# The seam between two attention layers: transposes, statistics and norm in another order, group values picked by a mask, and five unread products

## The chip, the cores and the metric

The kernel runs on one core of one Trainium2 chip. The metric is the device time of one execution in microseconds (us); lower is better. Three runs of the kernel before are known, and one more execution was profiled; the trace of that one gives every start time and duration below. Engines are named as the profile names them: PE is TensorE's matrix products (PEld its weight loads), DVE is VectorE, ACT is ScalarE, POOL is GpSimd, SP is the engine whose queue issues the transfers. A number like 1976.33 is a start in us from the beginning of the span.

## The reference

The input x has 128 rows of 256 positions with 256 channels. Two layers follow each other, and each adds an attention to its own input.

```python
# layer 0
x = x + L0(_gn(x), z, mask, ...)   # layer norm, 8 heads, bias from z, a gate, output product
# layer 1
x = x + L1(_gn(x), w_in, b_in, w_out, b_out, 16)  # 4 heads, keys within 16 positions

def _gn(v, G=32, eps=1e-5):
    B_, H_, W_, C_ = v.shape
    g = v.reshape(B_, H_, W_, G, C_ // G)
    m = jnp.mean(g, axis=(1, 2, 4), keepdims=True)
    s = jnp.var(g, axis=(1, 2, 4), keepdims=True)
    return ((g - m) / jnp.sqrt(s + eps)).reshape(v.shape)
```

What matters here is `_gn` ahead of layer 1. Its mean and variance are taken over all rows and positions of layer 0's output, for each of 32 groups of 8 channels. So no product of layer 1 can use its normalized input before the last row of layer 0 is known.

## The kernel before, in words

**Layer 0** works on pairs of rows, p from 0 to 63, in one loop in which four pairs are in flight: `now` (scores, exponentials, products with the values), `was` (gate, inverse sums, normalization), `old` (its second output row) and the pairs being loaded. Within a part of the code that is written under `manual_schedule` (the loop of layer 0 with its ending is one, layer 1 another), each engine runs its instructions in the order in which they are written. Between the parts a scheduler decides: in the built program the memsets of layer 1's accumulators, the constant masks, and also the two transposes at the head of layer 1 stand elsewhere than written. A finished output row is evicted by `keep_row` (line 1498), which adds the residual and writes it into `xo`, a tile of eight rows; when `xo` is full it is stored to DRAM (L1504), in x1. For each group of evicted rows `moments_of` puts work in a list, `later`: sixteen statistics instructions on DVE (L1519), and a merge of five small ones into the running statistics `st1` (L1528 to L1532). `some(n)` takes n entries off that list. The last eight rows form groups of four, two and two rows.

After the loop the last pair is still to be finished. The lines are `apply` (L1436 and L1444, products with the values and the sums of the exponentials), `gate` (L1451), `invert` (L1457), `spread` (L1475: TensorE spreads the inverse sums over the partitions, both rows in one PSUM tile), `normalize_last` (L1478), and then `out_row` (L1491) and `keep_row` for both rows. All statistics and merges that are left run after the last eviction.

**The seam.** `load_first` (L1559), issued within the loop, loads the first two rows of x1 into the memory of wq and wk, which layer 0 no longer needs. `turn` (L1901), written at the head of layer 1 but placed at 1963.91 and 1969.77 among layer 0's last instructions, transposes them into the memory of wv and wg, so that the first pair of layer 1 needs no load of its own behind the last store. `norm1` then does the norm: a product with the averaging matrix `avg` gives the mean of every group over the partitions (L1843); DVE forms the variance (L1853 to L1855); `spread_groups` copies each group's value to its eight channels (L1846), and four products with a single column (L1848) bring mean and variance to one value per partition for both halves of the channels; DVE adds the epsilon (L1858), POOL takes the power -0.5 (L1859), DVE forms nM1, the negative mean times that (L1860). `centre` (L1909) on ACT applies both to the transposed input, half by half.

**Layer 1** starts with a plain projection of pair 0 (L1984, L1999), with `nxt.centre` of pair 1 between its q and k evictions on ACT. Pair 1 and the later pairs are loaded from x1 (L1889, L1894) on SP's queue, transposed on DVE (L1904) and centred on ACT. The loop then overlaps a pair's attention with the next pair's projection by a method with seven products (L1956, L1960) whose operands are differences that POOL forms (L1922 to L1925). POOL also adds the bias to the residual (L1915) and masks the exponentials (L2024).

**The end.** The kernel also proves that its simplified arithmetic was allowed: `look` puts two half checks in a list, a maximum (L2128) and a comparison with its minimum (L2125, L2126). `some_checks(n)` takes n halves off the list, and the result is a verdict (L2288) by which a general kernel, which is not run here, would be chosen. Before the verdict stand the last pair's two output rows, evicted on DVE (L2100) and stored (L2106).

Of the kernel before, what the change touches and what calls it, by code (L numbers as in the profile page):

```python
# [9 lines left out]
F32 = mybir.dt.float32  # L10
# [763 lines left out]
def fast_kernel(  # L774
# [469 lines left out]
    class Pair:  # L1244
# [225 lines left out]
        def spread(self):  # L1470

            self.ps_rv = ps_s.tile([P, 2, KC, I], F32, name="ps_rv", tag="s")
            for r in range(2):
                for c in range(KC):
                    nc.tensor.matmul(self.ps_rv[:, r, c, :], head[:, r * KC + c, :], self.rv, start=True, stop=True)  # L1475

        def normalize_last(self, r):
            nc.vector.tensor_tensor(self.oT[r], self.oT[r], self.ps_rv[:, r], ALU.mult)  # L1478
# [75 lines left out]
    def load_first():  # L1554

        by_block = x1[0][0:2].rearrange("s (i b) (k j a) -> k j b (s i) a", b=D0, k=KC, a=D0)
        for k in range(KC):
            for j in range(HQ):
                nc.sync.dma_start(  # L1559
                    first[k][j * D0 : (j + 1) * D0].rearrange("b (i a) -> b i a", a=D0), by_block[k, j]  # L1560
                )

# [134 lines left out]
    with tc.manual_schedule():  # L1697
        old = was = Nobody()
        es = nn3 = None
        for p in range(NP):  # L1700
# [82 lines left out]
            old, was, now, nxt, nn = was, now, nxt, nn, nn3  # L1783
        was.apply(1, es)
# [3 lines left out]
        was.spread()  # L1788
        old.keep_row(1)
        for r in range(2):  # L1790
            was.normalize_last(r)
        for r in range(2):
            was.out_row(r)
            was.keep_row(r)
# [30 lines left out]
    with tc.tile_pool(name="l1", bufs=2) as sb, tc.tile_pool(  # L1825
# [11 lines left out]
        each = head.rearrange("p n d -> p (n d)").rearrange("p (n c) -> p n c", n=2)  # L1837
        wst = sb.tile([P, 4, 3, P], F32, name="wst", bufs=1)

        def norm1():  # L1840

            ps = [mm1("ps_gn") for _ in range(2)]
            nc.tensor.matmul(ps[0][:, :G], avg, st1[:, :, 1], start=True, stop=True)  # L1843

            def spread_groups(n, of):
                nc.vector.tensor_copy(each[:, n].rearrange("p (g e) -> p g e", e=GE), bcast(of, 2, GE))  # L1846
                for k in range(KC):
                    nc.tensor.matmul(  # L1848
                        ps[1][:, 2 * n + k : 2 * n + k + 1], each[:, n, k * P : (k + 1) * P], avg[:, 0:1],
                        start=True, stop=True,  # L1850
                    )

            nc.vector.tensor_tensor(dev, st1[:, :, 1], ps[0][:, :G], ALU.subtract)  # L1853
            nc.vector.tensor_mul(dev, dev, dev)
            nc.vector.scalar_tensor_tensor(dev, st1[:, :, 2], 1.0 / (S * NB * GE), dev, ALU.mult, ALU.add)  # L1855
            spread_groups(1, dev)
            spread_groups(0, st1[:, :, 1])
            nc.vector.tensor_scalar_add(R1c, ps[1][:, 2:4], 1e-5)  # L1858
            nc.gpsimd.tensor_tensor(R1c, R1c, mhalf[:, :KC], ALU.pow)  # L1859
            nc.vector.scalar_tensor_tensor(nM1, ps[1][:, 0:2], -1.0, R1c, ALU.mult, ALU.mult)  # L1860
# [15 lines left out]
        for n in range(2):  # L1876
            nc.vector.memset(o_eo[n], 0.0)
# [270 lines left out]
        with tc.manual_schedule():  # L2148
# [4 lines left out]
            for k in range(KC):  # L2153
                now.centre(k)
# [199 lines left out]
```

## Time and profile before

| what | us |
|---|---|
| median of three runs | 3128.2 (3127.22, 3128.6, 3128.2) |
| the profiled execution's own time | 3127.13 |
| its span, first to last instruction | 3125.4 |
| PE busy | 3014.3, 96% of the span |
| last eviction of layer 0 (L1498) starts | 1975.61 |
| store of the last eight rows (L1504) issued | 1976.33 |
| first product of the norm (L1843) | 1982.61 |
| nM1 (L1860) starts | 1987.17 |
| first centring (L1909) | 1987.42 |
| layer 1's first product (L1984) | 1988.29 |
| verdict (L2288) | 3118.46 |

The profiled execution's own time and its span differ by 1.7 us, which lie before the first and after the last instruction. The page gives busy times over the whole span; the stretch that the change touches is some 40 us of 3125, so it has to be read from the chain of waits (what the last instruction was released by, step by step), from the timeline (instructions in order of time, equal ones merged, with the idle time before them and what ended it) and from the table of windows (busy time, granted TensorE clock and DMA share of given stretches).

### The profile page before, as it was taken

To read this page: it belongs to the slowest core of one execution; us is meant where nothing else is said; L and a number is where in the kernel's file an instruction comes from. 1 tells how busy PE (TensorE), PEld (TensorE's weight loads), DVE (VectorE), ACT (ScalarE), POOL (GpSimd) and SP (SyncE) were. 2 spreads that over 40 slices of the span, in tenths; PEclk is the share of its full clock that TensorE was granted. 3 is DMA by queue.
4 is the path that set the end of the run, shared out by engine and by line. 5 is a ranking of instruction groups with operands and counts; after the bars stand their busy time and mean duration, and the time that the engine had idled before them with its cause. 6 is when DMAs were issued, how large, how long until landed. Compare 5 with 4: busy or idle time off the path is not lost.

```text
span 3125.4 us, 80592 instructions
## 1 busy us (share of the span) xinstructions
PE 3014.3 (96%) x33638; PEld 2097.3 (67%) x33638; DVE 2398.2 (77%) x4008; ACT 1575.7 (50%) x2639; POOL 2268.6 (73%) x1633
## 2 busy tenths in 40 slices
PE   5689999999999999999999999899999999999998
PEld 4355555566555556555555655688888888888886
DVE  7986677777777777777777777688878777777788
ACT  3454444444444444444444444355555555555553
POOL 3469899888889989888898987455555555555553
PEclk9799999999999999999999999999999999999999
DMA  9952433433333332333343332543434344444441
GB/s 359 390 180 52 99 72 97 99 68 91 91 99 71 98 99 68 91 91 99 70 98 99 64 94 68 118 97 90 97 90 96 91 96 91 95 92 93 94 95 50
DMA packets 690774, 327.90 MB, mean 105 GB/s; under 512 B 538624, under 2 KB 639872, under 8 KB 689248
## 3 DMA queue, kind: packets, MB, share of 16 engines
q1 hardware_dynamic: 686000, 320.02, 40.5%
q8 instruction: 266, 4.36, 0.6%
q10 hardware_dynamic: 4400, 2.63, 0.3%
q14 instruction: 108, 0.88, 0.1%
HBM read 253.83 MB, written 68.74 MB: 103 GB/s over the span
## 4 chain that ended last, share of the span: by engine, by line
PE 92%; DMA 4%; DVE 2%; POOL 1%; ACT 1%; issue 0%; SPq 0%; ACTq 0%; POOLq 0%; DVEq 0%
PE ps_p L1364 21%; PE ps_qk L1960 13%; PE ps_sc L1401 9%; PE ps_ov L1436 8%; PE ps_su_y L2092 7%; PE ps_y L1491 7%; PE ps_qk L1956 7%; PE ps_v L1382 7%; PE ps_o L2038 4%; PE ps_su L1444 3%; PE ps_sc L2013 3%; PE ps_su_y L2046 2%; DMA zt<-in_z_dram 2%; DMA xa<-in_x_dram 1%; PE ps_t L1143 1%; DVE st L1199 1%
## 5 line engine op out<-in xcount | busy, mean ns | idle before, releaser
L1425 POOL TENSOR_TENSOR eboth<-e 128x512 f32<-128x512 f32 x512 | 743.9, 1474 | 176.9 <-PE ps_su L1444 97.7
L1421 DVE TENSOR_TENSOR e<-ps_sc,eb 128x1024 f32<-128x1024 f32 x384 | 458.4, 1222 | 292.8 <-ACT ps_sc L1413 292.7
L1413 ACT ACTIVATE ps_sc<-ps_sc 128x1024 f32<-128x1024 f32 x384 | 375.5, 1007 | 438.7 <-PE ps_sc L1401 313.0
L1401 PE MATMUL ps_sc<-qT,kT 32*128 32x256 f32 x4096 | 294.8, 401 | 0.0
L1923 POOL TENSOR_TENSOR dT<-xgT,dT 128x256 f32<-128x256 f32 x63 | 46.1, 731 | 314.3 <-ACT xgT L1909 314.3
L2024 POOL TENSOR_TENSOR e<-e,bw 128x384 f32<-128x384 f32 x256 | 248.4, 1001 | 10.8 <-ACT e L2022 10.8
L2092 PE MATMUL ps_su_y<-w_out,oT 128*128 128x256 f32 x1008 | 254.5, 385 | 0.9 <-DVE sums L2063 0.9
L1401 PEld LDWEIGHTS ps_sc<-qT,kT 32*128 32x128 f32 x4096 | 185.9, 184 | 102.0 <-issue 91.4
L1491 PEld LDWEIGHTS ps_y<-wo,oT 128*128 128x128 f32 x1024 | 194.3, 190 | 87.6 <-issue 44.3
L1491 PE MATMUL ps_y<-wo,oT 128*128 128x256 f32 x1024 | 243.0, 380 | 6.6 <-POOL oT L1481 5.8
L1364 PE MATMUL ps_p<-xnT,wq 128*128 128x512 f32 x512 | 247.5, 605 | 0.1
L1436 PE MATMUL ps_ov<-e,v 128*32 128x256 f32 x4096 | 247.6, 382 | 0.0
L1364 PE MATMUL ps_p<-xgT,wg 128*128 128x512 f32 x512 | 247.3, 605 | 0.0
L1382 PE MATMUL ps_v<-wv,xnT 128*128 128x256 f32 x1024 | 241.8, 379 | 0.0
L1364 PE MATMUL ps_p<-xnT,wk 128*128 128x512 f32 x512 | 240.7, 592 | 0.0
L1382 PEld LDWEIGHTS ps_v<-wv,xnT 128*128 128x128 f32 x1024 | 194.5, 190 | 54.0 <-issue 30.9
L2069 DVE RECIPROCAL rv<-sums 128x256 f32<-128x256 f32 x128 | 223.1, 1743 | 0.1
L1969 ACT ACTIVATE u<-ps_qk,bin_c 128x256 f32<-128x256 f32 x378 | 174.9, 477 | 94.6 <-PE ps_qk L1960 94.6
L2092 PEld LDWEIGHTS ps_su_y<-w_out,oT 128*128 128x128 f32 x1008 | 181.8, 190 | 22.4 <-DVE sums L2063 1.3
L1436 PEld LDWEIGHTS ps_ov<-e,v 128*32 128x32 f32 x4096 | 120.0, 109 | 108.5 <-issue 41.8
L1364 PEld LDWEIGHTS ps_p<-xnT,wk 128*128 128x128 f32 x512 | 97.2, 190 | 122.8 <-issue 122.6
L1922 POOL TENSOR_TENSOR dT<-xgT 128x256 f32<-128x256 f32 x63 | 46.0, 730 | 183.2 <-ACT xgT L1909 183.2
(229 smaller groups left out, 6602.6 us busy)
## 6 DMA issues: line engine op xcount, KB each, us to landing
xa<-in_x_dram SPq DMA_DIRECT2D x8, 4096.0 KB
xt<-in_x_dram SPq DMA_DIRECT2D x64, 512.0 KB
x<-xo SPq DMA_DIRECT2D x16, 2048.0 KB
xt<-x SPq DMA_DIRECT2D x64, 512.0 KB
rvb<-rsum SPq DMA_DIRECT2D x252, 128.0 KB
xs<-x SPq DMA_DIRECT2D x252, 128.0 KB
out_dram<-yo SPq DMA_DIRECT2D x63, 512.0 KB
xs<-in_x_dram SPq DMA_DIRECT2D x248, 128.0 KB
```

The source lines that it names most:

```text
L1364: nc.tensor.matmul(ps, w[:, k, m * P : (m + 1) * P], getattr(self, src)[:, k, :], start=(k == 0), stop=(k == KC - 1),)
L1382: nc.tensor.matmul(self.ps_v[:, b * C : (b + 1) * C], self.xnT[:, k, t * P : (t + 1) * P], wv[:, k, :], start=(k == 0), stop=(k == KC - 1),)
L1401: nc.tensor.matmul(self.pss[q // 2][:, q % 2, b, :], self.kT[rs, c, r * I + b * P : r * I + (b + 1) * P], self.qT[rs, c, r * I : (r + 1) * I],
L1413: nc.scalar.activation(self.pss[a], ps, AF.Exp)
L1421: nc.vector.tensor_tensor(es[a], pss[a], eb[:, h : h + 2], ALU.mult)
L1425: nc.gpsimd.tensor_tensor(t, es[a][:, :, 0, :], es[a][:, :, 1, :], ALU.add)
L1436: nc.tensor.matmul(ov[q * D0 : (q + 1) * D0, c, :], self.v[:, r, b, h * D0 : (h + 1) * D0], es[q // 2][:, q % 2, b, :], start=(b == 0), st ...
L1491: nc.tensor.matmul(self.ps_y[:, b * C : (b + 1) * C], self.oT[r][:, k, b * P : (b + 1) * P], wo[:, k, :], start=(k == 0), stop=(k == KC - 1),)
L1960: nc.tensor.matmul(to, lhs, rhs, start=start, stop=True, skip_group_check=True)
L2024: nc.gpsimd.tensor_tensor(e[:, q], e[:, q], bcast(bw.rearrange("p b w -> p (b w)"), 1, KC), ALU.mult)
L2069: nc.vector.reciprocal(self.rv[:, r, :], self.sums)
L2092: nc.tensor.matmul(self.y[:, b], self.oT[r][:, k, b * P : (b + 1) * P], w_out[:, k, :], start=(k == 0), stop=(k == KC - 1),)
```

## The change

The change does seven things.

1. `turn_first` transposes the two loaded tiles after the loop of layer 0, ahead of the last pair's `apply` and `gate`; `turn` of pair 0 no longer does it.
2. `spread` fills one PSUM tile per row, and each row is normalized after its own half.
3. Of the statistics left, ten entries run before the eviction of row 0 of the last pair, the rest of that group and its merge before the eviction of row 1; only the last group and its merge run after it.
4. `norm1` no longer expands groups to channels. The variance is averaged over the partitions by a second product with `avg`, and a mask `own`, made once at the start by POOL, picks each partition's own group out of 32, by a multiplication and a sum over 64 elements. The epsilon and the scaling of the second moment are done ahead (`part`).
5. Five products of `avg` with columns of `w_in` go to a PSUM tile that nothing reads: two of 512 columns ahead of the norm's first product, one of 256 after it, two of 512 after its second.
6. The memsets of layer 1's accumulators, before placed by the framework between the last evictions, stand after the first centring's statements.
7. At the end two half checks are taken earlier, and the eviction of the last pair's row 0 stands after the checks instead of ahead of them.

```diff
-        def spread(self):
-            self.ps_rv = ps_s.tile([P, 2, KC, I], F32, name="ps_rv", tag="s")
-            for r in range(2):
-                for c in range(KC):
-                    nc.tensor.matmul(self.ps_rv[:, r, c, :], head[:, r * KC + c, :], self.rv, start=True, stop=True)
+        def spread(self, r):
+            self.ps_rv = ps_s.tile([P, KC, I], F32, name="ps_rv", tag="s")
+            for c in range(KC):
+                nc.tensor.matmul(self.ps_rv[:, c, :], head[:, r * KC + c, :], self.rv, start=True, stop=True)
...
+    def turn_first():
+        for k, w in enumerate((wv, wg)):
+            nc.vector.transpose(w.rearrange("p k c -> p (k c)"), first[k])
...
+        turn_first()
         was.apply(1, es)
         was.gate(1)
         was.invert()
         old.out_row(1)
-        was.spread()
         old.keep_row(1)
         for r in range(2):
+            was.spread(r)
             was.normalize_last(r)
-        for r in range(2):
-            was.out_row(r)
-            was.keep_row(r)
+        was.out_row(0)
+        some(10)
+        was.keep_row(0)
+        was.out_row(1)
+        some(len(later))
+        was.keep_row(1)
         some(len(later))
...
+        own = const.tile([P, KC, G], F32, name="own")
+        nc.gpsimd.memset(own, 1.0)
+        for sign, base in ((1, 0), (-1, GE - 1)):
+            nc.gpsimd.affine_select(
+                out=own, in_=own, compare_op=ALU.is_ge, fill=0.0,
+                base=base, pattern=[[sign * P, KC], [-sign * GE, G]], channel_multiplier=sign,
+            )
...
         def norm1():
             ps = [mm1("ps_gn") for _ in range(2)]
+            part = lrs[1][:, :G]
+            mine = head[:, 0, : KC * G].rearrange("p (k g) -> p k g", k=KC)
+            def take(to, of):
+                nc.vector.tensor_tensor(mine, own, bcast(of[:, :G], 1, KC), ALU.mult)
+                nc.vector.tensor_reduce(to, mine, AX.X, ALU.add)
+            spare = mm1("ps_spare", 1)
+            def busy(n):
+                nc.tensor.matmul(spare[:, :n], avg, w_in[:, 0, :n], start=True, stop=True)
+            for _ in range(2):
+                busy(512)
             nc.tensor.matmul(ps[0][:, :G], avg, st1[:, :, 1], start=True, stop=True)
-            def spread_groups(n, of):
-                nc.vector.tensor_copy(each[:, n].rearrange("p (g e) -> p g e", e=GE), bcast(of, 2, GE))
-                for k in range(KC):
-                    nc.tensor.matmul(
-                        ps[1][:, 2 * n + k : 2 * n + k + 1], each[:, n, k * P : (k + 1) * P], avg[:, 0:1],
-                        start=True, stop=True,
-                    )
+            busy(256)
+            nc.vector.tensor_scalar(part, st1[:, :, 2], 1.0 / (S * NB * GE), 1e-5, ALU.mult, ALU.add)
             nc.vector.tensor_tensor(dev, st1[:, :, 1], ps[0][:, :G], ALU.subtract)
             nc.vector.tensor_mul(dev, dev, dev)
-            nc.vector.scalar_tensor_tensor(dev, st1[:, :, 2], 1.0 / (S * NB * GE), dev, ALU.mult, ALU.add)
-            spread_groups(1, dev)
-            spread_groups(0, st1[:, :, 1])
-            nc.vector.tensor_scalar_add(R1c, ps[1][:, 2:4], 1e-5)
+            nc.vector.tensor_add(dev, dev, part)
+            nc.tensor.matmul(ps[1][:, :G], avg, dev, start=True, stop=True)
+            for _ in range(2):
+                busy(512)
+            take(m1, ps[0])
+            take(R1c, ps[1])
             nc.gpsimd.tensor_tensor(R1c, R1c, mhalf[:, :KC], ALU.pow)
-            nc.vector.scalar_tensor_tensor(nM1, ps[1][:, 0:2], -1.0, R1c, ALU.mult, ALU.mult)
+            nc.vector.scalar_tensor_tensor(nM1, m1, -1.0, R1c, ALU.mult, ALU.mult)
...
             for k in range(KC):
                 now.centre(k)
+            for t in (*o_eo, su_y):
+                nc.vector.memset(t, 0.0)
...
             was.out_row(1)
+            some_checks(1)
             now.apply(0)
...
             now.weigh(0)
+            some_checks(1)
             now.apply(1)
...
-            now.keep_row(0)
             some_checks(len(checks) + len(late))
             below(n_mask, cols[0], 1e8)
             tot = sm.tile([P, 1], F32, name="okmin", bufs=1)
             nc.vector.tensor_reduce(tot, ok.rearrange("p a n -> p (a n)"), AX.X, ALU.min)
+            now.keep_row(0)
```

More of the change, by code (lines that the diff above doesn't have):

```diff
@@ L1468, in fetch_sums @@
                 )
-        def spread(self):
-            self.ps_rv = ps_s.tile([P, 2, KC, I], F32, name="ps_rv", tag="s")
-            for r in range(2):
-                for c in range(KC):
-                    nc.tensor.matmul(self.ps_rv[:, r, c, :], head[:, r * KC + c, :], self.rv, start=True, stop=True)
+        def spread(self, r):
+            self.ps_rv = ps_s.tile([P, KC, I], F32, name="ps_rv", tag="s")
+            for c in range(KC):
+                nc.tensor.matmul(self.ps_rv[:, c, :], head[:, r * KC + c, :], self.rv, start=True, stop=True)
         def normalize_last(self, r):
-            nc.vector.tensor_tensor(self.oT[r], self.oT[r], self.ps_rv[:, r], ALU.mult)
+            nc.vector.tensor_tensor(self.oT[r], self.oT[r], self.ps_rv, ALU.mult)
         def normalize(self, r):
@@ L1836, in fast_kernel @@
         dev = lrs[0][:, :G]
-        each = head.rearrange("p n d -> p (n d)").rearrange("p (n c) -> p n c", n=2)
+        m1 = const.tile([P, KC], F32, name="m1")
+        own = const.tile([P, KC, G], F32, name="own")
[5 more added lines that the diff above has]
+            )
         wst = sb.tile([P, 4, 3, P], F32, name="wst", bufs=1)
@@ L1875, in fast_kernel @@
         su_eo = [su_y[:, n, 0] for n in range(2)]
-        for n in range(2):
-            nc.vector.memset(o_eo[n], 0.0)
-        nc.vector.memset(su_y, 0.0)
         class Pair1:
@@ L1899, in turn @@
                     self.xT = [w.rearrange("p k c -> p (k c)") for w in (wv, wg)]
-                    for k in range(KC):
-                        nc.vector.transpose(self.xT[k], first[k])
                     return
```

## The prediction

> **What bounds the kernel now.** I read the head of the page, then the chain of waits around the seam between the two layers, then the timeline there and at the end.
>
> ```profile
> span 3125.4 us, 80592 instructions
> ...
> PE 3014.3 (96%) x33638; PEld 2097.3 (67%) x33638; DVE 2398.2 (77%) x4008; ACT 1575.7 (50%) x2639; POOL 2268.6 (73%) x1633
> ```
>
> TensorE is busy 96% of the span. The diff leaves both loops alone, so only the seam (about 1964 to 2010 us) and the last 20 us can change. The chain across the seam:
>
> ```profile
> 1973.88 0.69 DVE xo L1498
> 1974.57 0.21 issue
> 1974.79 0.91 DVE ps_su_y L1878
> 1975.70 0.61 DVE xo L1498
> 1976.31 0.02 issue
> 1976.33 7.05 DMA x<-xo
> ...
> 1983.51 3.89 DMA xt<-x
> 1987.41 0.01 issue
> 1987.42 0.83 ACT xgT L1909
> 1988.24 0.04 issue
> 1988.29 9.06 PE ps_p L1984 x16
> ```
>
> The last eviction leaves at 1975.61, its store lands at 1983.38, and TensorE starts layer 1 only at 1988.29. The chain names the load of xt as what released the first centring (L1909). I don't believe it: the built program's list of waits has L1909 wait for the store x<-xo and for nM, not for that load. The timeline gives the other candidate:
>
> ```profile
> 1984.29 1.86 PE L1848 MATMUL ps_gn<-avg,head 128*128 128x1 f32 x8 [1.07 <-DVE head L1846]
> ...
> 1986.43 0.71 POOL L1859 TENSOR_TENSOR R1c<-R1c,mhalf 128x2 f32<-128x2 f32 x1 [22.79 <-DVE R1c L1858]
> ...
> 1987.17 0.16 DVE L1860 SCALAR_TENSOR_TENSOR nM<-ps_gn,R1c 128x2 f32<-128x2 f32 x1 [0.82 <-POOL R1c L1859]
> ...
> 1991.80 1.25 DVE L1904 STREAM_TRANSPOSE xT<-xs 128x1024 f32<-128x1024 f32 x1 [4.47 <-DMA xs<-x]
> ```
>
> nM ends at 1987.33, 0.09 us before L1909, while the store had been down for 4.0 us. So **the norm bounds the start of layer 1**. The last line matters later: pair 1's transpose waits for its load.
>
> ```profile
> 1978.00:1979.00 1.00, 0.00 (x0) 0.00 (x0) 0.90 (x6) 0.00 (x0) 0.00 (x0) 0.77 1.03 385
> ...
> 1992.00:1993.00 1.00, 1.00 (x4) 0.50 (x3) 1.00 (x1) 0.69 (x1) 0.00 (x0) 0.90 1.39 215
> ```
>
> In these one-microsecond windows the third number from the right is the granted TensorE clock. 0.77 puts a fall to 0.50 at 1978.54, 0.90 a return at 1992.2. Layer 1's first 16 matmuls take 9.06 us; 16 of the same shape take 7.06 at full clock (chain, 1932.23).
>
> [...] half clock lasted 13.66 us, four windows of 3.41. The window before the fall held 0.44 us of PE work; that from 1958.06 to 1961.48, with 1.73 us, cost nothing. [...]
>
> **The change, part by part.** Times are this profile's; orders come from the built programs.
>
> *Transposes ahead of the last gate.* Before, the copies from wq and wk ran at 1963.91 and 1969.77. Now both stand before the gate (L1451): statistics end 1963.91, merge 0.92, eviction 0.61, two transposes 0.62 each: gate at 1966.68 instead of 1966.40. The reciprocal goes from 1967.26 to 1967.30: +0.05. Cover: DVE's idle 0.27 and 0.18 there. Without it: 0.3. They wait for the loads of wq and wk; queued behind them are the gate and the reciprocal, for which TensorE's ps_rv waits. wk's load is down by then (DMA share 0.00 from 1962).
>
> *Sums spread by row.* Row 0 needs half of the eight ps_rv passes (1.99 us): ready at 1970.16, normalized from 1970.20 (the second buffer it takes has been free since the scores of 1958), ps_y from 1970.94 instead of 1971.85. Row 1 is normalized 1971.16 to 1971.81.
>
> *Statistics between evictions.* Sixteen take 2.13 us (1976.22 row), so 0.135 each. Ten: 1971.81 to 1973.16. Eviction of row 0 to 1973.77 (ps_y is done 1972.93). Six: 1974.58. Merge 0.92: 1975.50. Eviction of row 1 at 1975.50 instead of 1975.61, so the store lands at 1983.27 instead of 1983.38. The memsets (1.93 us) that stood between evictions now run after nM, under the wait for pair 1's load: nothing. What is left after the last eviction is one group, 2.16, and a merge to TensorE, 1.12: ps_gn at 1979.39 instead of 1982.61, **3.2 earlier**.
>
> *Mask instead of expanded groups.* Before, ps_gn to nM's end took 4.72 us. Now: first product to DVE 0.64; three steps at 0.23; to TensorE and back 0.25+0.6; masking 128x64 0.23 ([...] our 128x32 has 0.20); reduction 0.25 (okmin's 128x96); to POOL 0.08, power 0.71, nM 0.2: 3.65, so nM is there at 1983.0. The mean's mask step lies beside the second product. Both mask steps are absent from this trace: 0.4 to 1.0 us together. The mask's three POOL instructions run at the start, in front of 12.6 idle us: nothing.
>
> *Next late is the store*, 1983.27: L1909 waits for it anyway, at about 1983.33 instead of 1987.42, **4.1 earlier**. nM has 0.3 to spare.
>
> *Five spare products.* Two 128x512 after the last eviction (1.9 us), one 256 wide (0.45), two at the end (1.9, from about 1981.3 to 1983.2). The first pair waits for the last eviction, with ps_gn queued behind it, for which DVE waits; it is through at 1978.2, ps_gn is wanted at 1979.39. The last pair is ahead of layer 1 in TensorE's queue, but done before 1984.2, when the first centred half arrives. I take it that they hold the clock up.
>
> *How much of this reaches the loop.* TensorE from 1984.20: 0.27 for the second centred half, 6.9 and 3.45 of products: 1995.0. But ScalarE's queue has pair 1's centring ahead of q and k of the second half, and that waits for pair 1's load, which sits behind the store on SP's queue: 0.11 earlier only. Transpose 1991.69 to 1992.94, then ScalarE: centre 0.73, q 0.58, k 0.58, centre 0.73, v 0.5, v 0.5: 1996.6. scores(1) needs both v evicted: 1996.75, its third exponential ends at 1998.15, and pair 1's first product starts at 1998.20 instead of 2002.98: **4.8 earlier**. POOL follows: differences to 1997.8, bias to 2002.5, row 0 masked by 2004.4; TensorE wants it at 2005.8. So 1.2 us of the 6.0 that TensorE alone would gain stay with the load.
>
> *The end.* Two half checks move into DVE gaps: 0.46 into 1.12 idle us before 3106.96, 0.33 into the 0.40 before 3110.93. They leave the run from weigh to the last eviction:
>
> ```profile
> 3114.32 0.68 DVE L2100 TENSOR_TENSOR yo<-ps_y,xt 128x512 f32<-128x512 f32 x1
> ...
> 3117.84 0.68 DVE L2100 TENSOR_TENSOR yo<-ps_y,xt 128x512 f32<-128x512 f32 x1
> ...
> 3118.46 0.14 DVE L2288 TENSOR_SCALAR verdict<-ok_ps 1x1 int32<-1x1 f32 x1
> ```
>
> Row 0's eviction changes place within that run, which costs no time, but its store is issued at 3117.1 instead of 3115.04, close to row 1's. **0.8 earlier**; 0.3 if the stores collide, 1.0 at most.
>
> **Sum:** 4.8 + 0.8 - 0 = 5.6 us. The profiled execution took 3127.13 (span 3125.4 and 1.7 around it): 3121.5. The median stands 1.07 above it. If that spread comes from where the clock's windows fall in the seam, it goes with the change; if from elsewhere, it stays (3122.6). I take the middle, 3122.1.
>
> **Rivals.** *The clock falls all the same* (13%): between the first spare pair and the last lies a stretch 1978.2 to 1981.3 with one 256-wide product and two tiny ones. For it: 1.5 us of PE work in a window did not save the clock at 3108.36. Against: full cost needs half clock up to about 1988; a fall at 1982 that is mended by 1985.4 costs 0.7, which the wait for the load hides. Full cost, 1.95 us, ends TensorE at 1997.0, 3.9 earlier in the loop: gain 4.7 or less, 3122.4 to 3124. *The load is not the limit* (6%): if xs lands earlier than its record suggests, TensorE's own 6.0 remain: 6.8, 3120.4. *Slower* (3%): DVE is one queue, and now 3.1 us of statistics and two transposes stand before the last eviction; whatever holds it up moves store, loads and layer 1 one for one. Price one us per us of lateness; it decides from 5.6 us, that is wk's load landing after 1971.7. The idle DMA engines from 1962 speak against it. Time: 3130 for 7.5 us. That the change isn't carried out is excluded by the built order.
>
> **How the numbers follow.** About 0.2%, 6.3 us, is what a measurement of this kernel can tell from no change, so below 3121.9 counts as faster. The main case (78%; its own range 3121.0 to 3123.0) straddles that bound: 38% faster, 40% within. The clock rival adds 13% within, the load rival 6% faster, the slow one 2% slower and 1% within. Faster 44%, within 54%, slower 2%. Range 3120.4 to 3124.0, from the load rival to the clock rival.
>
> **What would show it.** Right: L1909's counterpart starts within 0.1 us of the store's landing, near 1983.3; granted clock 1.00 from there on; ScalarE idle for 4 us before pair 1's centring at 1993; first ps_qk near 1998.2. Wrong: nM later than the store; clock at 0.50 after 1984; ps_y of the last row later than the merge before it; a last eviction near 3117.8 less the seam's gain.

## The result and the profile after

| | us |
|---|---|
| before, median of 20 | 3127.44 (3124.45 to 3130.36) |
| after, median of 20 | 3122.35 (3117.61 to 3124.98) |
| after divided by before | 0.9984, 95% interval 0.9977 to 0.9990 |
| profiled execution of after | 3124.98, its span 3123.2 |

The change takes 5.1 us off the median, 0.16%; the prediction was 3122.1. A repeat of both kernels on another chip gave 3122.43 against 3126.61, 4.2 us. Single executions lie 3 to 5 us from their median at the extremes, and the profiled one of after is the slowest of its twenty: its span is only 2.2 us below the other's. The seam is therefore measured from marks inside it, not from the span.

The head of the page of after shows thirteen instructions more than before and TensorE about as busy as it was:

```profile
span 3123.2 us, 80605 instructions
...
PE 3020.6 (97%) x33642; PEld 2102.9 (67%) x33642; DVE 2397.7 (77%) x4010; ACT 1574.3 (50%) x2639; POOL 2267.1 (73%) x1636
```

The chain of waits of after across the seam (start, us, engine, tile, line):

```profile
1978.11 0.61 DVE xo L1497
...
1978.73 7.06 DMA x<-xo
...
1986.05 0.82 ACT xgT L1927
...
1986.91 7.13 PE ps_p L2002 x16
1994.05 3.45 PE ps_v L2017 x16
...
1999.68 4.17 PE ps_qk L1978 x18
```

The store is now on the chain right up to the first centring (L1927), and the 16 ps_p take 7.13 us where they took 9.06. (Below they are counted from the first ps_p to the first ps_v, which leaves out the end of the last one: 6.97 us against 8.90.) In the timeline of after, nM is there a full microsecond before the centring:

```profile
1984.88 0.16 DVE L1883 SCALAR_TENSOR_TENSOR nM<-m,R1c 128x2 f32<-128x2 f32 x1 [0.82 <-POOL R1c L1882]
1986.03 0.99 POOL L1890 TENSOR_TENSOR wst<-w_in 128x384 f32<-128x384 f32 x1 [1.18 <-DMA x<-xo]
1986.05 0.81 ACT L1927 ACTIVATE xgT<-wv,nM,R1c 128x512 f32<-128x512 f32 x1 [26.95 <-DMA x<-xo]
```

The middle line matters later: POOL starts to mix layer 1's weights when the store lands, not when its power is done.

All runs are compared by the same distances between starts, in us. "Gate" is the start of the last gate (L1451); ps_gn is the first product of the norm, nM its last step (nM1), ps_p the first product of layer 1 and ps_qk the first product of its loop. The first column is the distance from the gate before it; the rest count from the last gate, but for the last column, which is the whole way from the gate before the last to the first ps_qk.

| run | last gate | last eviction | ps_gn | nM | centring | ps_p | first ps_qk | whole |
|---|---|---|---|---|---|---|---|---|
| before | 10.65 | 9.21 | 16.21 | 20.77 | 21.02 | 21.89 | 36.58 | 47.23 |
| before_again | 10.64 | 9.21 | 16.21 | 20.76 | 21.00 | 21.87 | 36.42 | 47.05 |
| after | 12.28 | 9.04 | 13.01 | 15.90 | 17.06 | 17.93 | 30.70 | 42.98 |
| after_again | 12.28 | 9.03 | 12.99 | 15.88 | 17.09 | 17.96 | 30.72 | 43.00 |
| a: no spare products | 12.29 | 9.04 | 13.08 | 16.39 | 17.09 | 17.95 | 33.27 | 45.56 |
| b: spare products alone | 12.29 | 9.21 | 16.12 | 20.52 | 20.76 | 22.91 | 35.72 | 48.01 |
| c: old order of statistics | 11.03 | 8.04 | 14.97 | 18.08 | 19.12 | 19.98 | 32.75 | 43.78 |
| d: store split | 11.03 | 8.73 | 12.67 | 15.57 | 16.60 | 17.47 | 30.62 | 41.65 |
| e: old norm | 12.29 | 9.04 | 12.99 | 16.54 | 17.11 | 18.09 | 31.57 | 43.86 |
| f: old ending | 11.03 | 8.73 | 12.68 | 15.58 | 16.76 | 17.62 | 30.62 | 41.65 |
| g: split store, nM on POOL | 11.04 | 8.74 | 12.69 | 15.63 | 15.86 | 17.36 | 30.25 | 41.29 |
| h: as g, more spare products | 11.04 | 8.73 | 12.69 | 15.63 | 15.85 | 16.72 | 29.49 | 40.53 |
| h_again | 11.04 | 8.73 | 12.68 | 15.62 | 15.85 | 17.18 | 30.24 | 41.27 |
| k: as g, full seam | 11.04 | 8.74 | 12.70 | 15.63 | 15.87 | 16.75 | 29.50 | 40.53 |

The first column shows the clock as well as the work: in after, after_again, a, b and e the clock fell in the last pair of layer 0, and the gate came 1.25 us late in the kernels with the new order (12.28 against 11.03) and 1.64 in b, which has the old one (12.29 against 10.65). One-microsecond windows of after (the third number from the right is the granted clock):

```profile
1964.00:1965.00 1.00, 1.00 (x6) 0.84 (x5) 0.97 (x6) 0.00 (x0) 0.59 (x1) 0.82 0.00 0
...
1967.00:1968.00 1.00, 1.00 (x16) 0.41 (x11) 0.97 (x2) 0.00 (x0) 0.00 (x0) 0.50 0.00 0
```

Here it fell at 1964.64, and eight ps_y of that pair took 2.62 us instead of 1.99. TensorE waits 2.7 us for POOL's normalize just before (ps_y L1490), in every kernel that has no spare products there. Run f met no such window and is the changed kernel up to the first ps_qk. Timeline of before, then of f_old_tail (both gates and the first ps_qk):

```profile
1955.75 0.68 DVE L1451 SCALAR_TENSOR_TENSOR oT<-gT,ps_ov 128x512 f32<-128x512 f32 x1
1966.40 0.69 DVE L1451 SCALAR_TENSOR_TENSOR oT<-gT,ps_ov 128x512 f32<-128x512 f32 x1 [0.27 <-PE ps_ov L1436]
...
2002.98 1.99 PE L1960 MATMUL ps_qk<-xgT,w_in 128*128 128x256 f32 x8 [0.62 <-ACT e L2022]
```

```profile
1955.07 0.68 DVE L1451 SCALAR_TENSOR_TENSOR oT<-gT,ps_ov 128x512 f32<-128x512 f32 x1
1966.10 0.65 DVE L1451 SCALAR_TENSOR_TENSOR oT<-gT,ps_ov 128x512 f32<-128x512 f32 x1
...
1996.72 1.99 PE L1978 MATMUL ps_qk<-xgT,w_in 128*128 128x256 f32 x8 [0.62 <-ACT e L2040]
```

**The seam's gain is 47.23 to 41.65, 5.6 us** (f lost one window of 3.41 us to half clock in the seam itself, from 1980.81), and 4.2 where only the changed kernel loses clock in the last pair.

### The profile page after: what moved, and what is told of

It reads as the page before. It is cut to its first block, busy times and chain, and to the rows that moved or that the text cites. A ratio compares the mean times of both kernels' runs of the same rounds, so it can differ in the third digit from the quotient of the medians.

```text
span 3123.2 us, 80605 instructions
## 1 busy us (share of the span) xinstructions
PE 3020.6 (97%) x33642; PEld 2102.9 (67%) x33642; DVE 2397.7 (77%) x4010; ACT 1574.3 (50%) x2639; POOL 2267.1 (73%) x1636
## 4 chain that ended last, share of the span: by engine, by line
PE 92%; DMA 3%; DVE 3%; ACT 1%; POOL 1%; issue 1%; ACTq 0%; SPq 0%; POOLq 0%; DVEq 0%
PE ps_p L1364 21%; PE ps_qk L1978 12%; PE ps_sc L1401 9%; PE ps_ov L1436 8%; PE ps_y L1490 7%; PE ps_su_y L2110 7%; PE ps_qk L1974 7%; PE ps_v L1382 7%; PE ps_o L2056 4%; PE ps_su L1444 3%; PE ps_sc L2031 3%; PE ps_su_y L2064 2%; DMA xa<-in_x_dram 2%; DVE st L1199 1%; DMA zt<-in_z_dram 1%; PE ps_t L1143 1%
## 5 line engine op out<-in xcount | busy, mean ns | idle before, releaser
L1490 PEld LDWEIGHTS ps_y<-wo,oT 128*128 128x128 f32 x1024 | 195.5, 191 | 86.9 <-issue 44.2
L1490 PE MATMUL ps_y<-wo,oT 128*128 128x256 f32 x1024 | 244.7, 382 | 5.8 <-POOL oT L1480 5.8
```

The source lines that it names most:

```text
L1490: nc.tensor.matmul(self.ps_y[:, b * C : (b + 1) * C], self.oT[r][:, k, b * P : (b + 1) * P], wo[:, k, :], start=(k == 0), stop=(k == KC - 1),)
```

## The experiments

Twelve runs followed: nine other kernels, and three repeats. The theory was the prediction's: the order of the statistics brings the norm's start forward, the store then sets the first centring, and the spare products hold the clock through layer 1's first products.

**a_no_spare: the changed kernel without its spare products.**

```diff
-            for _ in range(2):
-                busy(512)
             nc.tensor.matmul(ps[0][:, :G], avg, st1[:, :, 1], start=True, stop=True)
-            busy(256)
...
-            for _ in range(2):
-                busy(512)
             take(m1, ps[0])
```

> The changed kernel without its five unread products. Measured inside the trace, since single runs of one kernel scatter by some us: from the start of the last gate of layer 0 to the start of the first ps_qk product of layer 1, 36.58 us before and 30.70 after. If the products hold TensorE's clock up, the clock falls here during the norm as it did before, the first 16 ps_p products take about 9.0 instead of 7.13 us and the interval is 32.6; the time is 1.9 us above the changed kernel. Rival, that the wait for pair 1's load hides a slow TensorE: the clock falls, but the interval stays at 31.5 or less. Rival, that the products hold nothing: clock 1.00 through the seam and 30.7.

Measured: 3123.51 (ratio 0.9988, 0.9981 to 0.9994); last gate to first ps_qk 33.27 instead of 30.70. The centring comes where it did (17.09), but the 16 ps_p take 9.52 us instead of 6.97. Windows of a_no_spare:

```profile
1979.00:1980.00 1.00, 0.00 (x0) 0.00 (x0) 1.00 (x10) 0.00 (x0) 0.00 (x0) 1.00 0.64 242
1981.00:1982.00 1.00, 0.23 (x2) 0.26 (x2) 0.66 (x5) 0.00 (x0) 0.00 (x0) 0.78 1.01 375
...
1990.00:1991.00 1.00, 1.00 (x2) 0.34 (x1) 0.00 (x0) 0.54 (x1) 0.00 (x0) 0.50 1.01 158
```

TensorE has nothing to do around 1979, and from 1981.57 to 1991.81 it runs at half clock. Its wait ahead of the norm's first product, in before, after and a_no_spare:

```profile
1982.61 0.60 PE L1843 MATMUL ps_gn<-st,avg 128*128 128x32 f32 x2 [7.04 <-DVE st L1532]
```

```profile
1981.99 0.41 PE L1871 MATMUL ps_gn<-st,avg 128*128 128x32 f32 x2 [1.19 <-DVE st L1531]
```

```profile
1981.77 0.61 PE L1864 MATMUL ps_gn<-st,avg 128*128 128x32 f32 x2 [4.77 <-DVE lrs L1865]
```

The changes of the clock lie on a grid of 3.41 us (in before, one fall that lasted from 268.46 to 271.87, and 327 such windows from 1992.2 to 3108.36), so the ends of the other windows can be counted. One ended 0.20 us ahead of ps_gn in a, 0.28 in after and 0.32 in after_again: the three lay alike, and only the kernel without the products lost its clock. The products are worth 2.6 us of the seam in this pair of executions and 1.2 us in the medians, where the intervals of the two ratios overlap. That they hold nothing, or that the load of pair 1 hides what they hold, is refuted.

**b_spare_alone: the kernel before with the five products and nothing else.**

```diff
+            for _ in range(2):
+                busy(512)
             nc.tensor.matmul(ps[0][:, :G], avg, st1[:, :, 1], start=True, stop=True)
+            busy(256)
...
             spread_groups(0, st1[:, :, 1])
+            for _ in range(2):
+                busy(512)
```

> The kernel before with only the five unread products added at the same places of its own norm. If they hold the clock: the 16 ps_p products take 7.1 instead of 9.06 us, the interval from the last gate to the first ps_qk is 34.6 instead of 36.58, the time 1.9 us lower. Rival: the norm before is longer than the gaps they fill, the clock falls all the same, 36.6.

Measured: 3126.37 (0.9999, 0.9991 to 1.0008); 35.72. In the old order TensorE still waits some four microseconds for statistics, the clock falls at 1982.89, and the last two products, now at half clock, stand ahead of layer 1. Timeline of b_spare_alone:

```profile
1985.89 3.76 PE L1846 MATMUL ps_spare<-w_in,avg 128*128 128x512 f32 x4
1987.29 0.81 ACT L1919 ACTIVATE xgT<-wv,nM,R1c 128x512 f32<-128x512 f32 x1 [30.66 <-DVE nM L1870]
...
1989.44 2.88 PE L1994 MATMUL ps_p<-xgT,w_in 128*128 128x512 f32 x6
```

The four records of the spare pair take 3.76 us instead of the 1.96 that they take at full clock; ps_p starts 2.15 us after the centring instead of 0.87. So **spare work is not free where it fails to hold the clock**: here it gave 0.9 of the interval instead of the 2.0 expected, and nothing that the times show.

**c_old_stats: the changed kernel with all statistics after the last evictions, as before.**

```diff
-        was.out_row(0)
-        some(10)
-        was.keep_row(0)
-        was.out_row(1)
-        some(len(later))
-        was.keep_row(1)
+        for r in range(2):
+            was.out_row(r)
+            was.keep_row(r)
```

> The changed kernel with all remaining statistics after the last eviction again. My working: the store leaves 0.7 us earlier, but the norm's first product is 2.5 us later, so nM and no longer the store releases the first centring, 1.5 us later than in the changed kernel; the gap between the first spare products and the norm grows to over 4 us, the clock may fall, up to 1.9 more: interval 32.2 to 34.1 against 30.70. Rival, that only the store counts: 30.0.

Measured: 3124.57 (0.9993, 0.9985 to 1.0002); 32.75, within what was expected. The centring comes at 19.12 instead of 16.76 in f, whose last gate is as undisturbed: the order of the statistics is worth 2.4 us there, although the last eviction itself is 0.7 earlier without it (8.04 against 8.73). Of the 2.4, 0.8 come from nM, which took 0.95 us in c (see d); that is part of why the centring came 2.1 after the changed kernel's instead of the 1.5 expected. Timeline of c_old_stats:

```profile
1983.22 1.00 POOL L1887 TENSOR_TENSOR wst<-w_in 128x384 f32<-128x384 f32 x1
1983.29 0.95 DVE L1880 SCALAR_TENSOR_TENSOR nM<-m,R1c 128x2 f32<-128x2 f32 x1 [0.82 <-POOL R1c L1879]
1984.32 0.81 ACT L1924 ACTIVATE xgT<-wv,nM,R1c 128x512 f32<-128x512 f32 x1 [27.76 <-DVE nM L1880]
```

By the medians the order is worth 2.2 us against 1.2 for the spare products (a), to the first ps_qk 2.1 (32.75 against f's 30.62) against 2.6: which of the two is worth more is not settled.

**d_split_store: six of the last eight samples stored a pair earlier,** to move the store out of the way.

```diff
-            if (s + 1) % GB == 0:
+            last = s // GB == S // GB - 1
+            if (s + 1) % GB == 0 or last and (s + 3) % GB == 0:
...
+                lo, hi = (0, GB) if not last else (0, GB - 2) if (s + 1) % GB else (GB - 2, GB)
...
+                    x1[j][lo:hi].rearrange("s (p b) c -> p s (b c)", b=NB),
+                    xo[:, lo * NB : hi * NB].rearrange("p (s b) c -> p s (b c)", b=NB),
```

> The changed kernel with the last eight rows stored in two pieces, six rows after the eviction before the last pair's and two rows at the end. If the landing of the store releases the first centring in the changed kernel, the centring here starts when nM is there, 0.9 us earlier; pair 1's load moves some 4 us ahead, so nothing but TensorE is left: interval 29.8 against 30.70. Rival, that the centring would have waited for nM or another semaphore anyway: 30.7.

Measured: 3121.40 (0.9982, 0.9975 to 0.9988); centring at 16.60, only 0.16 before f's, and 30.62 to the first ps_qk instead of the 29.8 expected, with one window at half clock from 1980.03. The store was out of the way, but nM took its place in an unforeseen manner. Timeline of d_split_store:

```profile
1980.68 1.00 POOL L1893 TENSOR_TENSOR wst<-w_in 128x384 f32<-128x384 f32 x1
1980.74 0.95 DVE L1886 SCALAR_TENSOR_TENSOR nM<-m,R1c 128x2 f32<-128x2 f32 x1 [0.82 <-POOL R1c L1885]
...
1981.78 0.81 ACT L1930 ACTIVATE xgT<-wv,nM,R1c 128x512 f32<-128x512 f32 x1 [25.24 <-DMA xt<-x]
```

nM, two columns wide, takes 0.95 us instead of 0.16, and ends with POOL's instruction that began 0.06 us before it. The centring starts 0.09 after nM ends; the load of xt that the last line names is not what it waited for. With the store down early, POOL no longer waits with the weights. The run c shows it too (0.95 beside 1.00), while in the kernel before nM took its mean from PSUM and needed 0.16 beside the same POOL instruction (1987.17 beside 1987.10). Taking the mean from SBUF, which the mask norm does, thus cost 0.8 us in c and d, beside that instruction; in the changed kernel POOL is still waiting for the store then, and nM takes 0.16. What makes the one wait for the other is not shown.

**e_old_norm: the changed kernel with the old norm,** the products kept.

```diff
+            spread_groups(1, dev)
+            spread_groups(0, st1[:, :, 1])
             for _ in range(2):
                 busy(512)
-            take(m1, ps[0])
-            take(R1c, ps[1])
+            nc.vector.tensor_scalar_add(R1c, ps[1][:, 2:4], 1e-5)
...
```

> The changed kernel with the old norm put back (groups expanded to channels, four single-column products); the five spare products, the spread sums and the order of the statistics stay. In the changed kernel the norm's end (nM) stood 1.16 us before the first centring. My theory: the old norm is 1.07 us longer by the prediction's count, so nM comes about as late as the store and the centring moves by 0 to 0.3 us; last gate to first ps_qk 30.7 to 31.0 at full clock (TensorE clock at 0.50 into layer 1 would add up to 2.6). Time 3122.3 to 3122.8, not told from the changed kernel. Rival: the mask is where the gain comes from, and then nM ends after +17.5, the centring moves by over 0.7 us and the interval is 31.5 or more, time 3123.2 or more.

Measured: 3122.39 (0.9985, 0.9979 to 0.9992). nM comes 0.64 us later (16.54), the centring 0.05 (17.11): **the mask norm is worth nothing that can be measured here**, since the store is later than either. The interval of 31.57 lies above the 31.5 of the rival, but not for its reason: the clock was at half from 1983.20 to 1986.62, and the 16 ps_p took 7.69. The old norm itself took 3.71 us here, from ps_gn to the end of nM; in before, at half clock, it had taken 4.72, and 4.55 in b. So some 1.0 of the 4.72 went with the clock, and the mask saves 0.65 against the old norm (3.06 in after), not 1.07.

**f_old_tail: the changed kernel with the old ending.**

```diff
-            some_checks(1)
             now.apply(0)
...
-            some_checks(1)
             now.apply(1)
...
+            now.keep_row(0)
             some_checks(len(checks) + len(late))
...
-            now.keep_row(0)
```

> The changed kernel with the old ending: the half checks at their old places and row 0 evicted after the last check. Seam as in the changed kernel: last gate to first ps_qk 30.5 to 31.0. From the eviction yo<-ps_su_y,xt to the verdict: 12.8 at full clock, as in the kernel with the spare products alone, instead of 12.2; at a fall of the clock in the ending up to 13.4. Time 0.5 to 0.6 us above the changed kernel, 3122.9. Prediction's own value: 0.8 above. Rival: the ending is bound by TensorE's last products and the change in it is worth nothing: the two verdict times are equal at equal clock.

Measured: 3121.88 (0.9984, 0.9977 to 0.9990) against 3122.9 expected, which does not tell it from the changed kernel. The trace does. From the last yo<-ps_su_y,xt to the verdict f needs 12.83 us and after_again 12.22, both with their last products at full clock. To the end of the span it takes 19.72 in f and 19.84 in b, and 19.12 to 19.74, 19.34 in the mean, in the nine executions with the new ending whose last products ran at full clock. The timeline of f_old_tail, then of after_again:

```profile
3111.38 0.25 DVE L2302 TENSOR_REDUCE okmin<-ok 128x1 f32<-128x96 f32 x1
3111.55 0.68 DVE L2118 TENSOR_TENSOR yo<-ps_y,xt 128x512 f32<-128x512 f32 x1
...
3112.17 0.14 DVE L2308 TENSOR_SCALAR verdict<-ok_ps 1x1 int32<-1x1 f32 x1
```

```profile
3112.04 0.25 DVE L2303 TENSOR_REDUCE okmin<-ok 128x1 f32<-128x96 f32 x1
3112.21 1.28 DVE L2118 TENSOR_TENSOR yo<-ps_y,xt 128x512 f32<-128x512 f32 x2
3113.41 0.14 DVE L2310 TENSOR_SCALAR verdict<-ok_ps 1x1 int32<-1x1 f32 x1
```

In after_again both rows leave back to back after the minimum, last thing before the verdict. The ending is worth 0.6 us at the verdict, where all nine show 12.22, and about 0.4 at the end of the span, where the two groups overlap.

**g_split_pool: d with nM computed by POOL,** so that nothing of the norm stands beside the weights.

```diff
             take(m1, ps[0])
+            nc.vector.tensor_scalar_mul(m1, m1, -1.0)
             take(R1c, ps[1])
             nc.gpsimd.tensor_tensor(R1c, R1c, mhalf[:, :KC], ALU.pow)
-            nc.vector.scalar_tensor_tensor(nM1, m1, -1.0, R1c, ALU.mult, ALU.mult)
+            nc.gpsimd.tensor_tensor(nM1, m1, R1c, ALU.mult)
```

> The split store (six of eight samples leave early), and nM computed on POOL right after the power, with the sign of the mean turned on VectorE beside it, so that no step of the norm shares its time with the mixing of the weights. Theory: in the split store's run the centring waited for nM, which took 0.95 us beside POOL's 1.00 us instead of 0.16. Without that, centring at gate +15.7 to +16.0 instead of +16.60, ps_p at about +16.8, last gate to first ps_qk 29.5 to 30.0 at full clock and up to 32 where it falls; time 0.5 to 1 us below the split store alone, 3120.5 to 3121. Rival: the multiplication on POOL costs what it saves (0.7 us, as the power there): centring at +16.4 or later and no gain.

Measured: 3119.81 (0.9977, 0.9969 to 0.9985), below the 3120.5 to 3121 expected and 1.6 us below d, of which the seam shows 0.4 (30.25 against 30.62) and the rest is not explained; the intervals of d and g overlap. Centring at 15.86. Timeline of g_split_pool:

```profile
1981.01 0.20 POOL L1887 TENSOR_TENSOR nM<-m,R1c 128x2 f32<-128x2 f32 x1
1981.24 0.81 ACT L1931 ACTIVATE xgT<-wv,nM,R1c 128x512 f32<-128x512 f32 x1 [24.50 <-POOL nM L1887]
```

POOL needs 0.20 for it and the centring follows 0.03 later: 0.74 us earlier than in d, as expected. The rival's price, 0.7 for a POOL instruction of this size, was that of the power, not of a multiplication. The interval is 30.25, just above the 30.0 expected at full clock: the clock was at half from 1979.78 to 1983.19, and the spare pair in front of ps_p took 3.48 us.

**h_all_fill, h_again: g with six more spare products,** in the wait of the last pair of layer 0 and in the ending.

```diff
+            if p == NP - 1:
+                spare0 = mm("ps_spare0")
+                for _ in range(2):
+                    nc.tensor.matmul(spare0, avg, w_in[:, 0, :512], start=True, stop=True)
             was.out_row(0)
...
             now.apply(0)
...
+            busy1(2)
...
+            busy1(1)
             for b in range(NB):
                 now.out_block(0, b)
+            busy1(1)
```

> As g, and more spare products with results nobody reads: two 512 wide ahead of the last pair's out_row in layer 0, where TensorE waits 2.7 us for POOL, and four in the ending (two after the first apply, one after the second, one after the first out_block). Theory: what is left of lost time around both ends is half clock in single executions: in the changed kernel's profile 16 products of the ending took 6.87 us and the last pair of layer 0 lost 1.7 us. Expected: granted clock 1.00 from 1950 to the verdict but for windows in which no more can be filled, verdict +12.2 after the eviction yo<-ps_su_y,xt, first ps_qk 29.5 to 30.0 after the gate, median 3119 to 3120.5, and executions that scatter less (range under 5 us instead of 7.4). Rival: the clock falls rarely enough that filling changes no median, or the spare products delay what is queued behind them: 3120.5 to 3122, verdict +12.5 or later.

> The kernel with all spare products once more, to see whether its full clock was the phase of the windows or the products. Theory: the products in the last pair and the ending hold the clock there in any phase; in the seam one window at 0.50 may return, as in g. Expected: gate before the last to the last gate 11.03 to 11.05, verdict +12.2 after the eviction yo<-ps_su_y,xt, gate to first ps_qk 29.5 without a fall and 30.2 to 30.6 with one. Median 3119.5 to 3120.5. Rival: a fall between 1960 and 1967 (gate distance 12.3) or in the ending (verdict over +12.5) as in the kernels without them.

Measured: 3120.24 (0.9978, 0.9971 to 0.9985) and 3120.45 (0.9981, 0.9973 to 0.9988). Both profiled executions have the last gate at 11.04 and the verdict at 12.22. The first kept the clock from 174 us to the ending, with the whole way at 40.53; the second lost one window in the seam (1981.77 to 1985.19) and took 41.27. The median is no better than g's and the scatter (3117.43 to 3122.26 in h, 3118.16 to 3122.29 in g) not smaller, so the rival holds for the times: what these products save is too small or too rare to be seen there. In the traces it is seen. A window of the clock ended 1.19 us after the start of the ps_y behind POOL's normalize in h, and the clock held; after_again and after, without the products, lost it with a window that ended 1.17 and 1.23 after that start. In the seam h and h_again are one kernel, and differ by where the window lay: it ended 1.26 us after ps_gn in h and 1.86 in h_again.

**k_full_seam: g with the two products in the last pair, and three instead of two in both groups of the seam.**

```diff
-            for _ in range(2):
+            for _ in range(3):
                 busy(512)
             nc.tensor.matmul(ps[0][:, :G], avg, st1[:, :, 1], start=True, stop=True)
...
-            for _ in range(2):
+            for _ in range(3):
                 busy(512)
```

> As g, with two spare products 512 wide in the last pair of layer 0 and three instead of two in both groups of 512 in the seam: TensorE was idle there for 1.17 us ahead of the norm's first product and for 0.8 us ahead of the first centred half. Theory: in g, d, f, c and e the clock still fell once in the seam, for one window, because some windows hold too little; fuller ones keep it. Expected: granted clock 1.00 from 1950 to 2000; ps_gn at gate +12.7 as in g (nothing delayed), 16 ps_p in 6.97, last gate to first ps_qk 29.5, and 40.5 to 40.6 from the gate before the last; time 0.3 to 0.7 us below g. Rival: the fall does not depend on such work: a window at 0.50 between gate +13 and +20 again, 30.2 or more. If it falls there, three products at half clock ahead of layer 1 make it 31 or more.

Measured: 3118.69 (0.9975, 0.9964 to 0.9987; seven runs), the lowest median of the study, though its interval overlaps g's; 29.50, and 40.53 the whole way; ps_gn at 12.70, so nothing was delayed. Windows of g_split_pool and of k_full_seam, at the same place of the seam (k is 2.05 us later):

```profile
1980.00:1981.00 1.00, 1.00 (x2) 0.34 (x1) 0.84 (x3) 0.00 (x0) 0.71 (x1) 0.50 0.87 305
```

```profile
1982.00:1983.00 1.00, 1.00 (x4) 0.47 (x3) 0.84 (x3) 0.00 (x0) 0.71 (x1) 1.00 0.81 281
```

The same microsecond of work holds four records at clock 1.00 and two at 0.50. One execution does not show that the clock cannot fall here when the windows lie otherwise. By the count of columns in the last section, an estimate, it would not: wherever a window is laid over this seam, it holds 1870 or more.

**after_again, before_again: both kernels unaltered, profiled once more.**

> The changed kernel, unaltered, once more: a second profiled execution and more times. Theory: its first profiled execution lost 1.25 us in the last pair of layer 0 to a window at half clock, which the kernel before's did not meet. Expected where that window is missing: gate before the last to first ps_qk 41.4 to 41.7 instead of 42.98 (47.23 in the kernel before); with it 43 to 43.9. In either, a fall of at most one window in the seam. Median 3122.0 to 3122.7. Rival: the 42.98 is what the change itself costs there, and it is seen again with the clock at 1.00.

> The kernel before, unaltered, in a second profiled execution, since the seam of before rests on one. Theory: its seam is slow in every execution, because TensorE has next to nothing to do from gate +12 to +21: granted clock at 0.50 there for two to four windows of 3.41 us, into the first layer-1 products; last gate to first ps_qk 35.5 to 36.6, and 47.2 from the gate before the last, or up to 48.9 where a window at 0.50 also meets the last pair of layer 0. Rival: the fall in the seam was a chance of that execution, and at full clock the interval is 34.6.

Measured: after_again 3122.43 (0.9986, 0.9979 to 0.9992), whole way 43.00 with half clock from 1962.81 to 1966.22, as in the first execution. That the 43.0 is the change's own cost is refuted by c, d and f, which have the same code in that pair and 11.03 to the gate at full clock, and by b. before_again: 47.05, and the seam at half clock from 1978.57 to 1992.23, as in the first. TensorE waited 7.04 us ahead of ps_gn in both, longer than two windows of 3.41 us, so that one window is empty wherever the windows lie.

## Why the prediction was right, step by step

The time was right to 0.3 us, and so near in part by luck. The 3122.1 stood 6.1 below the 3128.2 known then; the median of twenty was 3127.44, and the gain 5.1. Of the steps, most held, one term failed, the ending was worth half of what was said, and a loss of clock that both kernels can meet was missing.

- **What bounds the kernel, and the doubt about L1909's releaser:** held. With the norm earlier, the same centring is released by the store.
- **Transposes ahead of the gate:** the gate comes 0.38 us later at full clock (11.03 against 10.65); the prediction had 0.28, mended by the statistics that move away. The last eviction is 0.10 earlier than before (11.03 + 8.73 against 10.65 + 9.21), predicted 0.11.
- **Sums spread by row:** the last pair's ps_y starts 0.79 us earlier at full clock (15.31 after the gate before the last in f, 16.10 in before); predicted 0.91.
- **Statistics between evictions:** ps_gn 3.15 earlier from the gate before the last (23.71 in f against 26.86), predicted 3.2. The order of the statistics gives 2.29 of it (26.00 in c); the other 0.86 came with the spread sums and the memsets, less the transposes, and no run took one of these back alone.
- **Mask norm:** ps_gn to the end of nM takes 3.06 in after, and took 4.72; predicted 3.65. (The 0.23 for a masking step in it was the author's estimate; the two took 0.21 and 0.22.) The prediction put the whole difference down to the steps; e shows the larger part to be the clock. The prediction also said that the store comes next and leaves nM room; it left 0.75 us, not 0.3. So the shorter norm brings nothing (e).
- **The store sets the centring:** held in place, 3.9 earlier (27.79 in f against 31.67) instead of 4.1. From the store's landing to the centring ScalarE takes 0.26 us (three short steps in its queue, then the start, 1985.79 to 1986.05), where the prediction allowed 0.06.
- **The spare products hold the clock:** half right. That they would was the author's estimate. In after and after_again they do; in c, d, e, f, g and h_again the clock falls all the same, once, for a single window of 3.41 us. They cut the three windows at half clock of a to none or one. The clock rival's mechanism is thus common, but at its small price: up to 0.8 us (16 ps_p in 7.20 in f, in 7.69 in e, against 6.97), not 1.95.
- **How much reaches the loop** is the step that failed. (Its sum for TensorE makes 1994.8 and not 1995.0; the 6.0 agrees with 1994.8.) "So 1.2 us of the 6.0 that TensorE alone would gain stay with the load": none stay. From ps_p to the first ps_qk, after takes 12.77 us, and so does h, in which pair 1's transpose comes 3.92 us earlier (20.35 against 24.27 after the gate; 3.63 against 6.34 after ps_p): the load is not on the path, if only just. Its queue position was right, its duration wrong. From its issue to the transpose it took 7.86 us in before, and this value was carried over; after needed 6.90 and after_again 6.49. ScalarE's run behind that load, in the predicted order (centre, q, k, centre, v, v, from 1994.54) and predicted to end after TensorE's products, ended at 1998.16 in after, before its score products had (their exponentials wait 0.21 us for TensorE). By this reckoning, an estimate, a load of 7.86 us would have put it 0.96 later and on the path; that was not run. Timeline of after, then of h_all_fill:

```profile
1993.26 1.25 DVE L1922 STREAM_TRANSPOSE xT<-xs 128x1024 f32<-128x1024 f32 x1 [6.00 <-issue]
...
1999.68 1.99 PE L1978 MATMUL ps_qk<-xgT,w_in 128*128 128x256 f32 x8 [0.58 <-ACT e L2040]
```

```profile
1985.74 1.25 DVE L1930 STREAM_TRANSPOSE xT<-xs 128x1024 f32<-128x1024 f32 x1 [3.39 <-DMA xs<-x]
...
1994.88 1.99 PE L1986 MATMUL ps_qk<-xgT,w_in 128*128 128x256 f32 x8 [0.62 <-ACT e L2048]
```

- **The end:** 0.6 at the verdict at full clock and about 0.4 at the end of the span, predicted 0.8, with 0.3 for the case that the two rows' stores collide. Both executions of before lost clock in the ending as well (verdict at 13.3 instead of 12.8), and so did the first of after (13.04 instead of 12.22).
- **What was missing:** half clock in the last pair of layer 0. It costs the whole way some 1.6 us when it happens. It happened in both executions of after, in a, e and, with the old order, b, and in neither of before. Where the window lay tells the two groups apart: in these five it ended 1.17 to 1.45 us after the start of the ps_y behind POOL's normalize; in before, before_again, c, d, f and g it ended 0.78 to 1.00 ahead of that start, or 1.64 to 2.11 after it. TensorE's work and wait there are the same in all eleven, so this is a loss that the old kernel can meet as well as the new one, and not a cost of the change.

The sum by these sizes: 5.6 in the seam and 0.4 at the end is 6.0 where both kernels keep the clock in the last pair or both lose it; 4.2 and 0.4 is 4.6 where only the changed one loses it, as in the two profiled executions. The measured 5.1, and the 4.2 of the other chip, are below 6.0, though both intervals, of about 2 us on either side, hold it. What the rest is made of stays open.

## What to carry to other kernels

When a chain is shortened, take the durations of what comes next as a range: a DMA that took 7.9 us before took 6.5 to 6.9 in the changed kernel, and a limit argued from one record vanished. Spare TensorE work held the clock in after (16 ps_p in 6.97 us, against 9.52 without it), but where it left a thin window it failed, and then it stood, at half speed, in front of the work that it was to help (b: 3.76 us instead of 1.96). So measure the gaps, fill them, and ask of each place that a window can take what it would hold. Shorten the step that is late, and look at once for what is late next: here the norm's mask gained nothing behind a store, and splitting that store brought the centring forward by 0.2 us, and by 0.9 once the operation behind it no longer shared its time with POOL.

## What the runs showed of the hardware

- **A busy share does not tell, here, whether the clock falls.** The windows just before a fall held 1.22 us of PE records (after, last pair), 1.45 (b, there), 0.24 (b, seam), 2.01 (g) and 2.71 (e) of 3.41, and in h a window with the same 2.01 us passed (its place counted back from its next event in steps of 3.41), as did one with 1.73 in before (1958.06 to 1961.48).
- **A count of columns does tell it, here.** Count for each PE record the columns of its product (512 for 128x512), by the share of its time that lies in the window. From 1955 to 1990 the fourteen traces have 99 windows at full clock. The 15 after which the clock fell held 0 to 1483 columns; the 84 others held 1687 or more. So g's 2.01 us were 1384 columns and h's 1687; e's 2.71 us were 1369, since much of them was products one or 32 columns wide. In this stretch the two groups part between 1483 and 1687. That this holds elsewhere is not shown: in the ending of after the clock fell behind a window with 9216 columns (3104.69 to 3108.10), all of products with weights of 64x32 instead of 128x128.
- **A two-column VectorE operation took 0.8 us longer beside a POOL operation** when both its inputs lay in SBUF (nM, 0.95 us in c and d, against 0.16 with no POOL operation beside it in after), and no longer with one in PSUM (0.16 in before).
- **The same load of 128-byte packets took 7.8 us from issue to transpose in before, before_again and b, and 6.5 to 7.1 in all others,** c with its old order of statistics among them. Its packets took 15.7 to 17.0 ns in the mean in those three, and 12.9 in each of the others. What slows it was not tried; a, c, e and f each took one part of the change back, and the load stayed short, so that it goes with a part that no run took back (the transposes, the spread sums, the memsets) or with several together.
